# Layer 0 of a two-layer transformer kernel rebuilt: tokens tiled by head group, operands split into 12-bit halves, one ring of PSUM bank pairs

## The chip, the cores and the metric

The kernel runs on one core of one Trainium2 chip. The metric is the device time of one execution in microseconds (us); below full speed the profile gives the clock that was granted to TensorE as a share. The engines are called PE (TensorE; PEld are its weight loads), DVE (VectorE), ACT (ScalarE), POOL (GpSimd) and SP (SyncE, which only issues transfers).

## What is computed

Two layers over x of shape (2, 1024, 256), float32. Each layer normalizes x and adds an attention and a feed-forward network (FFN) of the same normalized input. The change touches layer 0 (layer 1 only in the order of its tokens):

```
def attn(x):                      # layer 0; b, t, e = 2, 1024, 256; h, d = 16, 16
    Q, K, V = ((x @ W.T).reshape(b, h, t, d) for W in (Wq, Wk, Wv))
    scores = causal(einsum('bhqd,bhkd->bhqk', Q, K))
    weights = softmax(scores / sqrt(d), axis=-1)
    ctx = einsum('bhqk,bhkd->bhqd', weights, V)
    return ctx.transpose(0, 2, 1, 3).reshape(b, t, e) @ Wp.T + bp
def ffn(x):
    w1, w2 = ternary(W_fc), ternary(W_proj)     # -s, 0 or s in groups of 64
    h = square(relu(x @ w1.T))                  # hidden width 1024
    return (h * rsqrt(mean(h * h) + eps)) @ w2.T
xn = layernorm(x)
x = x + attn(xn) + ffn(xn)
```

The reshape takes no transpose before it, so head h of a batch is made of the 64 tokens 64h to 64h+63, each cut into 16 pieces of 16 channels: 1024 positions of 16 numbers. Layer 1 is an attention with compressed keys and values and a second FFN.

## The kernel before

**Layout.** `x_sb` holds the 2048 tokens as 16 tiles of 128 consecutive ones. Layer 0 normalizes them, transposes them to channels by tokens (`xnT`, float32) and projects Q, K and V for a whole batch and 128 channels at a time (`project`, L252; float32, which PE runs as two records per matmul). A projection goes to DRAM ("rows") and comes back by `gather` (L279) in another order: for one *group* g of four heads (h4, h4 + 4, h4 + 8, h4 + 12 of a batch; eight groups in all) the heads lie at partitions 0, 32, 64 and 96, 16 rows each. This *quad* arrangement lets four matmuls with a contraction of 16 rows run side by side in PE's array (`tile_position`). A copy, mostly on POOL (L292), puts the positions of the gathered tile in order.

**The loop.** Everything in layer 0 runs under `tc.manual_schedule()`, so each engine executes its instructions in the order in which the loop writes them. The loop runs over groups g = -1 to 8 and over twelve *rounds* n. Round n takes a block of queries or keys of a width from `WIDTH` (512, 384, 256, 128, four times 512, and again 512, 384, 256, 128), in two *half-rounds* of two quads each. A half-round does two things at once, each with two of the four quads: `maxima` (L320) of group g + 1, that is, scores by query row, of which DVE takes the row maximum (L343 where no mask is needed, L338 with one); and `scores` (L358) of group g, that is, scores by key row, of which ACT takes exp (L375) and POOL clears the masked triangle (L378). `finish` (L347) transposes the negated maxima on PE (L352) and adds them to a 17th row of the queries, so that the scores come out with the maximum already subtracted. `product` (L386) multiplies weights and values two rounds later, in two parts where it is wide; `close` (L408) divides by the sum, and `project_out` (L423) applies Wp.

**PSUM.** Of eight banks, scores have two pairs (tag "s"), the product one bank ("o"), and three single banks ("m") serve maxima, transposes, FFN and output projection in turn.

**FFN.** `ffn` (L446) works on 512 tokens: eight `up` steps (L456; ReLU on ACT L462, square on DVE L463, sum of squares on POOL L468 and L469) and four `down` steps (L485; added to x at L492), the root of the mean square once per 512 tokens (L479). A list `fill` holds all of them with a cost, and a credit that the rounds earn decides when the next one is put in. The ternary weights are made in steps during g = -1 and 0 (`ternary`, L216).

**Order at the start.** All Q and K projections of batch 0 come first, then the gather of group 0, V, the gather of group 1, and batch 1's projections during g = -1.

Of the kernel before, what the change touches and what calls it, by code (L numbers as in the profile page):

```python
# [27 lines left out]
P = 128  # L28
# [22 lines left out]
def two_layers(ctx: ExitStack, tc: tile.TileContext, a: dict, out: bass.AP):  # L51
    nc = tc.nc
    x_d = a["x"].rearrange("(n p) e -> p n e", p=P)
# [8 lines left out]
    for g in range(4):  # L62
        nc.sync.dma_start(x_sb[:, 4 * g : 4 * g + 4, :], x_d[:, 4 * g : 4 * g + 4, :])
# [32 lines left out]
    def layernorm_T(scratch, xh, xl, ps_bank):  # L96
# [3 lines left out]
        for g in range(4):  # L100
# [7 lines left out]
            for n in range(4 * g, 4 * g + 4, 2):  # L108
# [12 lines left out]
                at = slice(n * P, (n + 2) * P)  # L121
                turned = pt.rearrange("p (c t) -> p c t", c=KC)
                nc.scalar.copy(xh[:, :, at], turned)
                nc.vector.tensor_tensor(xl[:, :, at], turned, xh[:, :, at], ALU.subtract)
# [12 lines left out]
    with ExitStack() as scope:  # L137
# [5 lines left out]
        GC = 4 * D0  # L143

        def ps_pair():
            return ps0.tile([P, 2, SC], F32, tag="s", name="ps_s", bufs=2)

        def ps_bank():
            return ps0.tile([P, SC], F32, tag="m", name="ps_m", bufs=3)

        def temp(name):
            return l0t.tile([P, SC], F32, tag="temp", name=name, bufs=6)

        wqkv = l0.tile([P, 3, KC, E], F32, tag="wqkv", name="wqkv")
        for i, key in ((1, "wk"), (0, "wq"), (2, "wv")):
            nc.scalar.dma_start(wqkv[:, i], a[key])
        wfc = l0.tile([P, KC, HID0], F32, tag="wfc", name="wfc")
        nc.gpsimd.dma_start(wfc, a["wfc"])
        wpr = l0.tile([P, HID0 // P, E], F32, tag="wpr", name="wpr")
        nc.gpsimd.dma_start(wpr, a["wpr"])  # L160
# [8 lines left out]
        nc.gpsimd.memset(half1[64:128, 64:128], 1.0)  # L169

        stage = []
        for i in range(3):
            t = l0.tile([P, H0, GC], F32, tag=f"stage{i}", name=f"stage{i}")
            nc.gpsimd.memset(t, 0.0 if i == 0 else 1.0)
            stage.append(t)

        nmx = []
        for k in range(2):
            t = l0.tile([P, TB, P], F32, tag=f"nmx{k}", name=f"nmx{k}")
            nc.gpsimd.memset(t, 0.0)  # L180
            nmx.append(t)

        xnT = main.tile([P, KC, B * S], F32, tag="xnT", name="xnT0")
        mv = l0.tile([P, NT, 2], F32, tag="ln_mv", name="ln_mv")
        rstd = l0.tile([P, NT], F32, tag="ln_rstd", name="ln_rstd")

        def ln_stats(g):
            for n in range(4 * g, 4 * g + 4):
                st = small.tile([P, 6], F32, tag="ln_st", name="ln_st")
                nc.vector.bn_stats(st, x_sb[:, n, :])  # L190
                nc.vector.bn_aggr(mv[:, n, :], st)
            r = rstd[:, 4 * g : 4 * g + 4]
            nc.scalar.activation(r, mv[:, 4 * g : 4 * g + 4, 1], AF.Sqrt, bias=eps["ln"])

        def ln_rstd(g):
            r = rstd[:, 4 * g : 4 * g + 4]
            nc.vector.reciprocal(r, r)

        def ln_turn(n):

            pt = ps_bank()
            for k in range(2):
                xn = l0t.tile([P, E], F32, tag="xn", name="xn", bufs=3)
                nc.vector.tensor_scalar(
                    xn, x_sb[:, n + k, :], mv[:, n + k, 0:1], rstd[:, n + k : n + k + 1],
                    ALU.subtract, ALU.mult,
                )
                for kc in range(KC):
                    nc.tensor.transpose(
                        pt[:, (2 * kc + k) * P : (2 * kc + k + 1) * P],  # L210
                        xn[:, kc * P : (kc + 1) * P], ident,
                    )
            nc.scalar.copy(xnT[:, :, n * P : (n + 2) * P], pt.rearrange("p (c t) -> p c t", c=KC))


        def ternary(w):  # L216
# [3 lines left out]
            def begin():  # L220
                t["wb"] = l0t.tile([P, SC], BF16, tag="q_wb", name="q_wb", bufs=1)
# [30 lines left out]
        def project(b, i, m, n=None):  # L252
            if (b, i, m) not in pend:
                pend[b, i, m] = ps_pair()
# [370 lines left out]

# [486 lines left out]
```

## Time and profile before

| what | value |
|---|---|
| median of 3 runs (lowest, highest) | 1468.72 us (1468.25, 1474.49) |
| the profiled execution | 1462.64 us |
| its span, first to last instruction | 1460.9 us |
| layer 0: start to the first maxima (L327) | 0 to 64.7 us |
| maxima of group 0 alone (g = -1) | 64.7 to 124.2 us |
| groups 0 to 6: scores of g, maxima of g + 1 | 124.2 to 564.6 us |
| group 7: scores alone | 564.6 to 605.6 us |
| last output projection ends | 615.4 us |
| layer 1 | 615.4 to 1460.9 us |
| mean granted clock of PE | 0.925 |

A line of the profile names the line of the kernel, the engine, the operation, what it writes and reads (`out<-in`) with shapes, how often it ran, its busy time, the mean duration of one in ns, and after the second bar the idle time of its engine just before it and what ended that. A timeline line has start, duration, engine, line, operation and tiles. In a table of stretches each engine's busy time is followed by its number of instructions. Matmuls overlap, and one that waits for a free bank can look busy.

### The profile page before, as it was taken

How to read it: one execution, taken by the hardware profiler on the slowest of the kernel's cores; microseconds unless marked ns; L12 is line 12 of the kernel's file. 1: busy time of each engine (PE TensorE's matmuls, PEld its weight loads, DVE VectorE, ACT ScalarE, POOL GpSimd, SP SyncE). 2: the span in 40 equal slices, each digit the busy share in tenths (PEclk: the TensorE clock that was granted, in tenths of full speed). 3: DMA queues.
4: the chain of work that ended last, by engine and by line, in shares of the span. 5: the costliest groups of instructions: out<-in, count | busy, mean ns of one | idle time of the engine just before them, and what ended most of it. 6: DMA issues, size and time to landing. Idle time of an engine off the chain costs nothing.

```text
span 1460.9 us, 36203 instructions
## 1 busy us (share of the span) xinstructions
PE 1355.2 (93%) x15382; PEld 818.7 (56%) x15382; DVE 828.3 (57%) x2161; ACT 591.5 (40%) x1131; POOL 530.3 (36%) x557
## 2 busy tenths in 40 slices
PE   5799999999999999865996899999999999999998
PEld 2334354354455344354874566767668566766676
DVE  2366555554554653273241577777665877776654
ACT  1113444443443544322330544444455544444453
POOL 2258671540612331127430532232345321323342
PEclk9786899998999999677996999999999999999999
DMA  5311000100100000130006000000000000000000
GB/s 193 105 57 45 1 22 1 23 21 2 23 1 9 1 1 1 42 95 0 30 29 162 8 3 14 3 14 13 13 14 24 4 11 13 11 6 13 13 13 20
DMA packets 56578, 39.26 MB, mean 27 GB/s; under 512 B 36896, under 2 KB 52512, under 8 KB 56064
## 3 DMA queue, kind: packets, MB, share of 16 engines
q1 hardware_dynamic: 50800, 29.47, 6.9%
q10 hardware_dynamic: 4944, 3.41, 0.8%
q0 software_dynamic: 672, 4.06, 0.7%
q8 instruction: 121, 1.98, 0.6%
q14 instruction: 41, 0.34, 0.1%
HBM read 24.35 MB, written 10.49 MB: 24 GB/s over the span
## 4 chain that ended last, share of the span: by engine, by line
PE 80%; DVE 6%; POOL 4%; issue 4%; ACT 3%; DMA 2%; ACTq 0%; SPq 0%; DVEq 0%; POOLq 0%
PE ps_s L921 17%; PE ps_m L327 13%; PE ps_o L965 11%; PE ps_t L870 7%; PE ps_o L398 5%; PE ps_m L485 5%; PE ps_m L456 4%; PE ps_t L989 4%; PE ps_s L259 4%; PE ps_s L368 2%; DVE p L927 2%; PE ps_o L755 1%; PE ps_m L435 1%; PE ps_t L954 1%; POOL qa L766 1%
## 5 line engine op out<-in xcount | busy, mean ns | idle before, releaser
L934 ACT ACTIVATE p<-p,nmax 128x1024 f32<-128x1024 f32 (+7 forms) x256 | 198.4, 775 | 326.3 <-DVE nmax L927 324.0
L921 PE MATMUL ps_s<-kT,qc 128*128 128x512 f32 (+3 forms) x768 | 307.1, 511 | 7.4 <-DVE nmax L927 7.0
L327 PE MATMUL ps_m<-head,head 16*128 16x512 f32 (+3 forms) x768 | 231.5, 571 | 6.9 <-DVE nmx L338 4.7
L375 ACT ACTIVATE p<-ps_s 128x1024 f32<-128x1024 f32 (+1 forms) x192 | 154.2, 810 | 199.0 <-PE ps_s L368 194.7
L939 DVE STREAM_TRANSPOSE pT<-p 128x1024 f32<-128x1024 f32 (+7 forms) x256 | 197.8, 772 | 0.2 <-ACT p L934 0.2
L921 PEld LDWEIGHTS ps_s<-kT,qc 128*128 128x128 f32 x768 | 125.6, 189 | 110.1 <-issue 64.7
L368 PE MATMUL ps_s<-head,head 17*128 17x512 f32 (+3 forms) x768 | 182.8, 587 | 1.0 <-ACT p L375 1.0
L965 PE MATMUL ps_o<-pT,vrep 32*64 32x128 f32 x9216 | 181.8, 279 | 1.9 <-DVE xT L974 1.8
L965 PEld LDWEIGHTS ps_o<-pT,vrep 32*64 32x64 f32 x9216 | 137.7, 130 | 70.8 <-issue 62.2
L888 POOL TENSOR_TENSOR qc<-t,t 32x512 f32<-32x512 f32 x128 | 161.8, 1264 | 8.2
L327 PEld LDWEIGHTS ps_m<-head,head 16*128 16x128 f32 x768 | 88.7, 193 | 119.8 <-issue 44.3
L946 POOL COPY rb<-rinv 128x512 f32<-128x512 f32 x32 | 19.6, 611 | 372.8 <-DVE rinv L944 338.2
L927 DVE CUSTOM_DVE_ANT_0 p<-ps_s,zeros 128x512 f32<-128x512 f32 x128 | 87.6, 684 | 70.5 <-PE ps_s L921 70.0
L378 POOL TENSOR_SCALAR_AFFINE_SELECT p<-p 128x256 f32<-128x256 f32 x128 | 55.0, 441 | 170.6 <-ACT p L375 170.2
L927 DVE CUSTOM_DVE_ANT_0 p<-ps_s,maskz 128x512 f32<-128x512 f32 (+3 forms) x128 | 62.3, 486 | 77.7 <-PE ps_s L921 77.5
L343 DVE TENSOR_REDUCE nmx<-ps_m 128x1 f32<-128x512 f32 x128 | 82.6, 686 | 34.8 <-PE ps_s L368 30.1
L398 PE MATMUL ps_o<-p,v 128*32 128x512 f32 (+4 forms) x920 | 93.8, 483 | 0.6 <-POOL p L378 0.5
L927 DVE CUSTOM_DVE_ANT_0 p<-ps_s,maskz,nmax 128x512 f32<-128x512 f32 (+3 forms) x128 | 70.5, 551 | 19.5 <-PE ps_s L921 2.6
L338 DVE CUSTOM_DVE_ANT_0 junk<-ps_m,maskz,nmx 128x512 f32<-128x512 f32 (+3 forms) x128 | 65.5, 548 | 28.2 <-PE ps_s L368 19.8
L456 PE MATMUL ps_m<-xnT,wfc 128*128 128x512 f32 x128 | 74.2, 709 | 1.3 <-DVE nmx L338 1.3
L884 POOL TENSOR_TENSOR t<-t,sinq 128x512 f32<-128x512 f32 x32 | 40.7, 1270 | 91.1 <-ACT t L883 87.4
L338 DVE CUSTOM_DVE_ANT_0 junk<-ps_m,maskz 128x512 f32<-128x512 f32 (+3 forms) x128 | 57.5, 486 | 24.7 <-PE ps_s L368 13.6
(185 smaller groups left out, 1944.1 us busy)
## 6 DMA issues: line engine op xcount, KB each, us to landing
rows<-proj SPq DMA_DIRECT2D x12, 512.0 KB, 2.6
stage<-rows SPq DMA_DIRECT2D x96, 64.0 KB, 2.4
x_sb<-in_x SPq DMA_DIRECT2D x4, 512.0 KB, 11.4
wo<-in_wo SPq DMA_DIRECT2D x8, 256.0 KB, 3.1
x<-x_sb SPq DMA_DIRECT2D x4, 512.0 KB, 2.8
xin<-x SPq DMA_DIRECT2D x16, 128.0 KB, 3.1
out<-xin SPq DMA_DIRECT2D x16, 128.0 KB, 1.7
w<-in_w ACTq DMA_DIRECT2D x2, 768.0 KB, 5.0
```

Of the source, the lines that this page charges most:

```text
L327: nc.tensor.matmul(t[:, :w], quad(q, c, D0)[:, i * P : (i + 1) * P], quad(k, c, D0)[:, k0 : k0 + w], start=True, stop=True, tile_position= ...
L338: nc.vector.tensor_tensor_reduce(junk[:, :w], t[:, :w], maskz[:, SC - w :], -1.0, dst if k0 else 3.0e38, ALU.add, ALU.min, dst,)
L368: nc.tensor.matmul(t[:, c % 2, :w], quad(k, c, D0 + 1)[:, j * P : (j + 1) * P], quad(q, c, D0 + 1)[:, at : at + w], start=True, stop=True, ...
L375: nc.scalar.activation(p[:, pair[0] : pair[0] + 2, :w], t[:, :, :w], AF.Exp)
L398: nc.tensor.matmul(quad(box["o"], c)[:, SC - w + lo : SC - w + hi], values[g][:, j, 32 * c : 32 * c + 32], p[:, c, lo:hi], start=(j == 0), ...
L456: nc.tensor.matmul(ph, wfc[:, kc, hc * P : (hc + 1) * P], xnT[:, kc, n * SC : (n + 1) * SC], start=(kc == 0), stop=(kc == KC - 1),)
L888: nc.gpsimd.tensor_tensor(qc[b, i][64 + 32 * x : 96 + 32 * x, g, hh], t1[at : at + 32], t2[at : at + 32], ALU.add,)
L921: nc.tensor.matmul(sc[:, : n1 - n0], qc[s.b, s.i][:, s.g, h // QP, h % QP, :], kT[:, s.b * S + n0 : s.b * S + n1], start=True, stop=True,)
L927: nc.vector.tensor_tensor_reduce(s.p[:, n0:n1], sc[:, : n1 - n0], mask, -1.0, 3.0e38 if n0 == 0 else s.nmax, ALU.add, ALU.min, nmax,)
L934: nc.scalar.activation(p[:, :w], p[:, :w], AF.Exp, bias=nmax, scale=-1.0, accum_out=rsum)
L939: nc.vector.transpose(s.pT[:, : s.nsb, h, :], p[:, : 32 * s.nsb])
L965: nc.tensor.matmul(s.o[64 * hh : 64 * hh + 64, c, : QP * 32], vrep[32 * c : 32 * c + 32, s.b * 32 + sb, :], s.pT[32 * c : 32 * c + 32, sb, ...
```

## The change

**Token order.** A tile pair of `x_sb` now holds the 256 tokens of one group of heads. x is loaded by 32 DMAs of 64 tokens from SP's and ACT's queues. Projection, attention and FFN of layer 0 all work per group of 256 tokens. Layer 1 gets its usual order back when it transposes, and reads and writes by strided access.

**Halves.** The normalized input and the Q, K and V weights are split into two float32r parts, a 12-bit upper half and the rest (`xh`, `xl`, `halves`). A projection is four products of halves, one record each. For Q and K both halves go through DRAM and come back stacked: 16 rows of upper and 16 of lower halves per quad, 32 in all. Head times head gives upper x upper plus lower x lower; a second matmul against a copy with the halves exchanged (`swap`, eight DMAs from SBUF to SBUF, or for group 0 a second gather) gives the mixed terms. Scores have a third matmul, a row of ones against the split maxima (`top`). V is projected with tokens as rows, and its heads are gathered by four DMAs straight into `values`.

**PSUM.** Maxima and scores take bank pairs from one ring of three ("ms"). One bank ("m") serves all else, one ("o") the products, which are no longer split.

**FFN.** Weights are float32r (a ternary value fits into one half), inputs and hidden values are halves. Each group has four `up` and four half `down` steps. Square and sums move to POOL and ACT, and the reciprocal root is made from ScalarE's Ln and Exp with one correction step on DVE, once per group.

**Order.** A dictionary `plan` puts each step at a fixed place: group, round, after the first ("x1") or second ("x2") half-round; what such a step still has to do on DVE or ACT is done by `settle` after the next half-round's reductions and exps. Projections of groups 0 and 1 come before the loop, of 2 to 4 in g = -1, of 5 to 7 in groups 0 to 2.

```diff
         def ps_pair():
-            return ps0.tile([P, 2, SC], F32, tag="s", name="ps_s", bufs=2)
+            return ps0.tile([P, 2, SC], F32, tag="ms", name="ps_ms", bufs=3)
...
-            return ps0.tile([P, SC], F32, tag="m", name="ps_m", bufs=3)
+            return ps0.tile([P, SC], F32, tag="m", name="ps_m")
...
+        def project(g, i, bank=ps_bank, lower=nc.gpsimd):
+
+            pw = bank()
+            for m in range(2):
+                four_ = [(kc, x, s) for kc in range(KC) for x in (xl, xh) for s in (1, 0)]
+                for n, (kc, x, s) in enumerate(four_):
                     nc.tensor.matmul(
...
+            nc.scalar.activation(t[:, 0, :].bitcast(F32R), pw, AF.Copy, scale=scale)
+            if lower is nc.vector:
...
+                nc.scalar.activation(t[:, 1, :], pw, AF.Copy, scale=scale)
+                nc.gpsimd.tensor_tensor(t[:, 1, :], t[:, 1, :], t[:, 0, :], ALU.subtract)
...
+                st = l0t.tile([P, H0, GC], F32, tag="stage", name="stage", bufs=1)
+            src = rows[g, i].rearrange("s m (j d) t -> s d (m j) t", d=D0)
             for c in range(4):
...
+                for s in range(2):
+                    lo = 32 * c + D0 * s
+                    q.dma_start(st[lo : lo + D0], src[1 - s if swapped else s, :, :, at])
...
+            for c in range(4):
+                for s in range(2):
+                    lo, of = 32 * c + D0 * s, 32 * c + D0 * (1 - s)
+                    nc.sync.dma_start(swapped[lo : lo + D0].bitcast(F32), t[of : of + D0])
...
+            for c in range(4):
+                src = rows[g, 2][c // 2, GC * (c % 2) : GC * (c % 2) + GC, :]
+                src = src.rearrange("t (j d) -> (t j) d", d=D0).rearrange("(k p) d -> p k d", p=P)
+                nc.sync.dma_start(values[g % 2][:, :, c, 0:D0], src)
...
+            k, q = heads[g, 1], (heads[g, 0], heads[g, 0, "swapped"])
+            t = ps_pair()
+
+            def run(part):
+                for c in pair:
+                    nc.tensor.matmul(
+                        t[:, c % 2, :w], quad(q[part], c)[:, i * P : (i + 1) * P],
+                        quad(k, c)[:, k0 : k0 + w],
+                        start=(part == 0), stop=(part == 1), tile_position=(32 * c, 0),
+                    )
...
+                if k0 + w < (i + 1) * P:
+                    nc.vector.tensor_reduce(
+                        peak(g)[:, i, pair[0] : pair[0] + 2], t[:, :, :w], AX.X, ALU.max, negate=True
+                    )
+                    return
...
+                    if part < 2:
+                        of, by = quad(k[part], c)[:, j * P : (j + 1) * P], quad(q, c)[:, at : at + w]
+                    else:
+                        of, by = quad(onesr, c, 2), quad(tops[g, iq], c, 2)[:, SC - w :]
...
+            whole = l0t.tile([P, SC], F32, tag="whole", name="whole", bufs=1)
+            nc.scalar.activation(whole, ph, AF.Relu)
+            nc.gpsimd.tensor_tensor(whole, whole, whole, ALU.mult)
...
+                nc.scalar.copy(t[:, 0, :], whole)
+                nc.scalar.activation(sq, whole, AF.Square)
+                nc.gpsimd.tensor_tensor(t[:, 1, :], whole, t[:, 0, :], ALU.subtract)
+                if j:
+                    nc.gpsimd.tensor_tensor(acc, acc, sq, ALU.add)
...
+            def add():
+                if k == 0:
...
+                    nc.scalar.activation(r, v, AF.Ln)
+                    nc.scalar.activation(r, r, AF.Exp, scale=-0.5)
...
+        for g in range(NG):
+            at(g, 0, "x1", lambda u=g: down(u, 0, 0))
+            at(g, 0, "x2", lambda u=g: down(u, 0, 1))
+            at(g, 1, "x1", lambda g=g: box["turn", g, 1]())
+            at(g, 2, "x1", lambda u=g: down(u, 1, 0))
+            at(g, 2, "x2", lambda u=g: down(u, 1, 1))
...
+            at(g, 7, "x1", lambda g=g: close(g, 0))
+        for g in range(-1, NG - 1):
+            at(g, 5, "x1", lambda g=g: box["turn", g + 1, 0]())
+            for j in range(4):
+                at(g, 8 + j, "x2", lambda u=g + 1, j=j: up(u, j))
+        for g in range(3):
+            at(g, 4, "x2", lambda g=g: project(g + 5, 1))
+            at(g, 5, "x2", lambda g=g: project(g + 5, 0))
+            at(g, 6, "x2", lambda g=g: project_v(g + 5))
...
+                        for r in range(3):
+                            for runs, _ in both:
+                                if r < len(runs):
+                                    runs[r]()
+                        for _, f in both:
+                            f()
+                        settle()
+                        if part == 0 and k >= 0:
+                            product(k // 12, k % 12)
+                        place(g, n, "x2" if part else "x1")
...
                             nc.tensor.matmul(
                                 pw[:, i * SC : (i + 1) * SC], w[:, kc, hc * P : (hc + 1) * P],
-                                x[:, kc, n * SC : (n + 1) * SC],
+                                x[:, kc, n * SC : (n + 1) * SC].rearrange(
+                                    "p (c h t) -> p h c t", c=2, h=4
+                                ),
```

As built, the instruction stream of the changed kernel has a table load before each of the eight Ln and each of the eight Exp of the FFN.

## The prediction

> **What bounds the kernel now.** I read the busy shares first, then a table of stretches cut where layer 0 changes its work (first maxima at 64.7 us, first scores at 124.2, last maxima at 564.6, last product at 605.6), then the timeline of one round, then the groups of instructions.
>
> ```profile
> PE 1355.2 (93%) x15382; PEld 818.7 (56%) x15382; DVE 828.3 (57%) x2161; ACT 591.5 (40%) x1131; POOL 530.3 (36%) x557
> ```
> ```profile
> core 0: us, PE busy (x) PEld busy (x) DVE busy (x) ACT busy (x) POOL busy (x), PEclk, DMA share, GB/s
> 0.00:64.70 64.70, 37.34 (x96) 18.04 (x96) 20.30 (x57) 10.03 (x16) 10.97 (x27) 0.89 0.41 146
> 64.70:124.20 59.50, 56.45 (x149) 24.15 (x149) 35.88 (x91) 10.18 (x14) 36.89 (x34) 0.76 0.23 74
> 124.20:564.60 440.40, 433.65 (x2770) 201.04 (x2768) 243.06 (x682) 186.96 (x255) 184.20 (x216) 0.92 0.05 11
> 564.60:605.60 41.00, 39.34 (x240) 13.88 (x236) 2.74 (x8) 20.01 (x28) 6.83 (x17) 0.71 0.00 1
> ```
> TensorE is busy throughout the loop, and nobody else is above 55% of it. Seven groups take 440.4 us, 62.9 each; the last, with scores alone, takes 41.0.
>
> ```profile
> 300.73 0.70 PE L327 MATMUL ps_m<-head,head 16*128 16x512 f32 x2
> 300.74 0.70 PE L368 MATMUL ps_s<-head,head 17*128 17x512 f32 x2
> 301.26 0.59 PE L327 MATMUL ps_m<-head,head 16*128 16x512 f32 x2
> 301.27 0.59 PE L368 MATMUL ps_s<-head,head 17*128 17x512 f32 x2
> 301.80 0.64 PE L398 MATMUL ps_o<-p,v 128*32 128x256 f32 x8
> 302.37 1.26 PE L327 MATMUL ps_m<-head,head 16*128 16x512 f32 x3
> 302.94 0.70 PE L368 MATMUL ps_s<-head,head 17*128 17x512 f32 x2
> ```
> One float32 matmul is two records, and four quads run side by side: a half-round of 512 columns takes 301.80 - 300.73 = 1.07 us. The third maxima record then stands from 302.37 to 302.94 for a bank that VectorE frees: a "busy" PE can be a waiting one. The same timeline gives 0.85, 0.62 and 0.41 us for 384, 256 and 128 columns: 0.054 us per pass and 128 columns, plus 0.1 per set of records. A group's 24 half-rounds make 12 x 1.06 + 4 x (0.85 + 0.62 + 0.41) = 20.2 us. Products (0.99, 0.78, 0.57, 0.36 by width) make 9.4 and their splits 1.1, FFN up 16 x 0.48 = 7.7, down 32 x 0.228 = 7.3, six blocks of four transposes 3.6, the sums of squares 0.5: 49.8 us. Of the 13 left to 62.9, five are the granted clock (0.92), some two the output projection; the rest, six, is waits for banks.
>
> Float32r, as the change uses it, is in layer 1's FFN:
>
> ```profile
> 705.05 3.12 PE L755 MATMUL ps_o<-w3t,hid 128*128 128x256 f32 x24
> 708.01 0.40 PE L740 MATMUL ps_wide<-xl,w2t 128*128 128x512 f32 x1
> 708.24 0.39 PE L740 MATMUL ps_wide<-xh,w2t 128*128 128x512 f32 x1
> ```
> One record per matmul, every 0.23 us for 512 columns and 2.96/24 = 0.123 for 256. The drains of a round:
>
> ```profile
> L343 DVE TENSOR_REDUCE nmx<-ps_m 128x1 f32<-128x512 f32 x112 | 72.3, 686 | 32.9 <-PE ps_s L368 30.1 <-PE ps_m L327 2.1
> L338 DVE CUSTOM_DVE_ANT_0 junk<-ps_m,maskz,nmx 128x512 f32<-128x512 f32 x28 | 19.9, 748 | 5.7 <-PE ps_s L368 4.0 <-PE ps_m L327 1.6
> L375 ACT ACTIVATE p<-ps_s 128x1024 f32<-128x1024 f32 x84 | 85.9, 1024 | 109.1 <-PE ps_s L368 106.3 <-POOL p L378 1.5 <-POOL acc L469 1.2
> L469 POOL TENSOR_TENSOR acc<-acc,sq 128x512 f32<-128x512 f32 x28 | 35.9, 1281 | 2.2
> L479 ACT ACT_TABLE_LOAD x4 | 5.1, 1283 | 0.1
> ```
>
> **The change, part by part, for a group at full clock.** Maxima and scores: three sets of one pass instead of two sets of two. Per half-round 3 x 0.054 per 128 columns plus 0.2 (today's) to 0.3 (0.1 per set); the middle gives 0.90, 0.74, 0.58, 0.41, so 17.7 us (16.5 to 18.9): only 2.5 saved, since the third set, which brings the maximum in, eats most of it. Products 9.4 (no splits). Up and down: 32 records each of 0.123, 3.9 and 3.9, and 0.95 for the sums of squares now made in every group: 6.7 saved. Four blocks of transposes 2.4 (values come through a DMA). Sum 38.3. In groups 0 to 2 three projections of 16 records add 5.9; today all projections lie before group 0.
>
> The waits: the ring of three pairs is handed out as maxima, scores, maxima, and so on; the scores of a half-round take the pair of the maxima one half-round before, so their first set waits for that reduction. Without a mask it is one instruction of 128x1024, not in this trace: at least one L343 (0.69), at most two (1.37); VectorE's copy of that size out of PSUM (L272) took 1.22, which I take as the nearest. Masked ones follow each other every 0.67, 0.54, 0.40, 0.27 us, two per half-round. Matmul end to VectorE's start and back adds 0.27 (0.17 of it the fill within a record). Against this stand the last score set (0.15 to 0.3), the product (first half) and whatever the plan puts there. Half-rounds with too little: rounds 4 to 7 without projections (0.6 + 1.2, 0.2 + 1.2, 0.2 + 1.2, 1.2), rounds 1 and 3 (1.1, 0.7), rounds 8 and 9 (0.8): about 8 us per group, 5 where projections fill in.
>
> A second wait is new: the transposes of the maxima in round 1 need the one bank "m", which holds the first FFN output until it is added. That add waits behind two reductions, exp (0.81), a table load (L479's 1.28), Ln (0.26), a second load (1.28), Exp (0.26), four small VectorE operations (0.6) and the add (0.48): some 5.6 us after the maxima, covered by 0.6 of PE work. Queued behind the transposes stands the whole of TensorE; behind Ln every exp. I take 5 us in each of 8 groups (bounds 0, were the loads hidden, and 7). Smaller waits for "m" behind ScalarE's copies: 1.5.
>
> Other engines per group: ScalarE 24 exps 19, FFN 12 x 0.6, copies 2.4, tables 3, projections 3: 35. POOL 16 selects 6.8, 11 FFN operations (1.05 to 1.28) 13.4, two permutes of 1.98, bias 1.5, lower halves 2.5: 28. VectorE 28. SP issues 39 DMAs of 0.45: 17. All lie beside PE's 44, if their order holds. The copies of the lower halves and the 64-byte value gathers have some 30 us of cover; uncovered, a gather of 8 issues plus 2.4 to land would cost 6 us.
>
> The clock: low in stretches of quads and products with few full-array matmuls; in layer 1's float32r stretch 708 to 736 us it is 1.00. Between 0.92 and 1.00 I take 0.95: 2 us per group. Groups 0 to 2: 38.3 + 5.9 + 5 + 5 + 1.5 + 2 = 57.7; 3 to 6: 38.3 + 8 + 5 + 1.5 + 2 = 54.8; output projection, mostly inside ring waits, 2 in all. Sum 394, against 440.4 (bounds: 7 x 38.3 + 17.7 = 286 without any wait; 448 with today's 62.9 and 1 more).
>
> Before the loop: SP and ScalarE now issue 35 loads; ScalarE's 18 (0.45 to 0.5) end near 10 us and hold its first square root until 11.5, so the first transposes stay near 13. Two projections, rows out, then 16 gathers of 0.5 on ScalarE's queue, behind a wait for the rows at 26: until 35 the next group's root and copy stand behind them, and VectorE and PE behind those. Then a chain of transposes, copies, four projections, ternary steps: first maxima near 58 (48 to 66) against 64.7. Next stretch: maxima in two sets 12.6, nine projections 17.7, up 3.9, transposes and scales 4.6: 38.8, at a clock of 0.9 and with POOL at 40 us taken as 45 (39 to 56) against 59.5. Last group: scores 17.7, products 9.4, down 4.9, transposes and output 6.6, the chain 5, and 3.5 for the clock (0.71 today): 47 (38 to 56) against 41.0. Tail: 8 against 9.8. Layer 1, 845.5 us from 615.4, has only its addresses and eight stores changed: nothing, hidden behind matmuls (0 to 3).
>
> Sum: 58 + 45 + 394 + 47 + 8 + 845.5 = 1397.5 of span against 1460.9. 1.7 us lie around the span, and the median of the runs is 6.1 above the profiled 1462.6: 1405 us.
>
> **The skill against the trace.** The trace has VectorE's reductions at 0.69 us per 512 columns whatever TensorE does. The Trainium skill (TensorEngine Tiling, PSUM Bottleneck) says that tiling speeds TensorE up but not the emptying of PSUM; that speaks against this change, and taken strictly (every half-round at reduction plus hand-over, some 43 us per group before all else) it gives about what I have for the ring. In the last group PE is busy 39.34 of 41.00 us at a granted 0.71. The skill (TensorE: Matmul & The Clock Gate, What's actually happening) says that a busy array is released to the full clock; the trace differs, and by the page the last group would be some 3 us shorter than I say.
>
> **Rivals.** (1) The waits are covered: half the ring's and the chain's cost gone, groups of 46 to 48, loop 330, first maxima at 50: near 1325. For it: table loads run ahead of their wait (L479's did). Against: nothing but 0.6 us lies in front of round 1's transposes. (2) POOL leads in rounds 8 to 11: two selects and three FFN operations, 4.4 us, against PE's 3.3, and "whole" has one buffer, so the next ReLU waits for POOL and the exps behind it: 4 x 1.1 x 8 groups = 35: 1440. Against: rounds 4 to 7 leave POOL nearly idle. (3) Slower: the ring. If the hand-over costs 0.9 us a half-round more, because ScalarE or the settling adds stand in front of the reductions, 24 x 0.9 x 7 = 150: 1555; it decides from 65 us per group on, where the loop's growth eats the 17 us won around it. For it: ScalarE at 35 of 55 us. Against: today VectorE starts within 0.1 us of the records' end. (4) The single passes bring nothing in quads: half-rounds stay 1.06, 3 more per group, 1430; layer 1's rows speak against it.
>
> **How the numbers follow.** Forecast (1360 to 1425) 0.45; rival 1 0.20; rivals 2 and 4 0.20; rival 3 0.12 slower, and 0.03 within half a per cent (7 us, about what a measurement here can tell from no change). Faster 0.83 to 0.85, rounded down for what I overlooked: 0.82, same 0.03, slower 0.15. Range 1320 to 1470, from rival 1's lower part to where rival 2's cost is met by a late first maximum.
>
> **What would show it.** Groups 55 to 58 us apart (by the transposes of the maxima); one PE stall near 5 us per group there; a half-round of 512 columns in 0.85 to 0.95 us; first maxima at 48 to 66 us; clock above 0.92. A group over 65 us, with PE waiting for the reductions, makes the forecast wrong; so does one under 48.

## The result, and the profile after

The changed kernel took 1556.74 us (median of 4 runs, 1548.56 to 1562.0) beside 1470.83 for the kernel before on the same chip: 1.058 of it, 95% interval 1.052 to 1.064. It is slower; the forecast was 1405. The profiled execution has a span of 1560.3 us. (The 1468.72 given ahead is the median of three runs of the kernel before, 1470.83 that of four.)

The first line is the busy shares on the page, the others the table of stretches, cut at the same events as before (first maxima, first scores, last group's first scores, last output projection); after each stretch stand its length, the busy time of each engine, the granted clock and the DMA share.

```profile
PE 1312.1 (84%) x15998; PEld 890.1 (57%) x15998; DVE 818.2 (52%) x2113; ACT 654.7 (42%) x1247; POOL 538.5 (35%) x575
```
```profile
core 0: us, PE busy (x) PEld busy (x) DVE busy (x) ACT busy (x) POOL busy (x), PEclk, DMA share, GB/s
0.00:82.00 82.00, 21.60 (x116) 18.21 (x116) 27.30 (x53) 16.62 (x28) 19.76 (x35) 0.79 0.41 112
82.00:170.60 88.60, 54.49 (x297) 40.21 (x296) 41.93 (x111) 22.00 (x41) 39.15 (x32) 0.68 0.34 82
170.60:641.90 471.30, 398.82 (x3141) 242.31 (x3140) 219.04 (x618) 225.43 (x326) 173.65 (x220) 0.78 0.21 40
641.90:703.00 61.10, 49.25 (x358) 29.21 (x358) 6.28 (x18) 28.86 (x42) 14.55 (x26) 0.81 0.00 1
703.00:1560.30 857.30, 787.96 (x12091) 560.12 (x12089) 523.66 (x1315) 361.81 (x811) 291.38 (x265) 0.94 0.08 24
```

PE went from 93% to 84% busy, and what is left runs at a lower clock: 0.78 in the loop, against 0.92. Every stretch is longer than before:

| us | before | forecast | after | after less forecast |
|---|---|---|---|---|
| to the first maxima | 64.7 | 58 | 82.0 | 24.0 |
| g = -1 | 59.5 | 45 | 88.6 | 43.6 |
| groups 0 to 6 | 440.4 | 394 | 471.3 | 77.3 |
| group 7 and tail | 50.8 | 55 | 61.1 | 6.1 |
| layer 1 | 845.5 | 845.5 | 857.3 | 11.8 |
| span | 1460.9 | 1397.5 | 1560.3 | 162.8 |

**Before the loop.** ACT's timeline (start, duration, engine, line; "ACTq" is the issuing of transfers):

```profile
4.12 18.70 ACTq L67 DMA_DIRECT2D x_sb<-in_x  x13
24.21 0.29 ACT L240 ACTIVATE ln_rstd<-ln_mv,eps_ln 128x2 f32<-128x2 f32 x1
38.98 9.26 ACTq L349 DMA_DIRECT2D ctx_n<-rows  x16
48.29 0.29 ACT L240 ACTIVATE ln_rstd<-ln_mv,eps_ln 128x2 f32<-128x2 f32 x1 [13.43 <-DMA ctx_n<-rows]
```

Thirteen loads of x hold the queue for 18.7 us, 1.4 each: the chain of waits shows the issue itself standing for earlier loads (12.3 us at one of them). The first square root comes at 24.2; the next group's stands behind rows and gathers until 48.3.

**In g = -1** the waits of PE name one source first, POOL's normalized input (two operations of 1.22 us on a queue that also does ternary steps):

```profile
PE ps_e L256 <- POOL xn L249: 13.2, 4, 6.3
PE ps_m L256 <- POOL xn L249: 11.8, 4, 8.0
```

**In the loop** the list of PE's waits (total us, times, longest) is led by the transposes of the maxima:

```profile
PE ps_m L438 <- DVE x_sb L607: 33.8, 7, 5.3
PE ps_ms L459 <- DVE peak L413: 9.7, 14, 1.0
PE ps_ms L459 <- DVE peak L420: 7.4, 14, 0.7
PE ps_m L577 <- POOL h L563: 7.1, 6, 1.2
PE ps_m L577 <- ACT whole L552: 6.6, 7, 1.2
```

The timelines of PE, POOL and ACT in group 5, which starts at 509.4, show the sequence:

```profile
513.11 0.74 PE L577 MATMUL ps_m<-wpr,h 128*128 128x256 f32 x4
515.05 0.74 PE L577 MATMUL ps_m<-wpr,h 128*128 128x256 f32 x4 [1.19 <-POOL h L563]
516.28 1.76 PE L587 MATMUL ps_m<-ones,acc 128*128 128x1 f32 x8 [0.49 <-POOL acc L565]
519.23 0.66 PE L483 MATMUL ps_o<-p,v 128*32 128x128 f32 x8
524.64 1.09 PE L438 MATMUL ps_m<-ident,nmx 128*128 128x128 f32 x4 [4.75 <-DVE x_sb L607]
```
```profile
511.94 1.05 POOL L553 TENSOR_TENSOR whole<-whole 128x512 f32<-128x512 f32 x1
513.73 1.27 POOL L563 TENSOR_TENSOR h<-whole,h 128x512 fp32r<-128x512 f32 x1 [0.38 <-ACT h L561]
514.95 1.27 POOL L565 TENSOR_TENSOR acc<-acc,sq 128x512 f32<-128x512 f32 x1
```
```profile
520.17 1.28 ACT L599 ACT_TABLE_LOAD   x1
521.46 0.20 ACT L599 ACTIVATE rn<-rn 128x2 f32<-128x2 f32 x1
521.68 1.28 ACT L600 ACT_TABLE_LOAD   x1
522.98 0.20 ACT L600 ACTIVATE rn<-rn 128x2 f32<-128x2 f32 x1
```

Down waits for POOL, the sums take 1.76 us for eight records of one column, and the transposes wait 4.75 us for the add behind Ln and Exp. From 516 to 533 the granted clock is 0.5. Rounds 0, 1 and 2 take 9.1, 8.7 and 8.2 us (means over the seven groups) at clocks of 0.89, 0.53 and 0.56; the other nine rounds take 2.5 to 6.1 us.

### The profile page after: what moved, and what is told of

Read it like the earlier page. It is cut to its first block, busy times and chain, and to the rows that moved or that the text cites. A ratio compares the mean times of both kernels' runs of the same rounds, so it can differ in the third digit from the quotient of the medians.

```text
span 1560.3 us, 37942 instructions
## 1 busy us (share of the span) xinstructions
PE 1312.1 (84%) x15998; PEld 890.1 (57%) x15998; DVE 818.2 (52%) x2113; ACT 654.7 (42%) x1247; POOL 538.5 (35%) x575
## 3 DMA queue, kind: packets, MB, share of 16 engines
q1 hardware_dynamic: 102192, 43.90, 12.3%
## 4 chain that ended last, share of the span: by engine, by line
PE 66%; DVE 10%; POOL 9%; ACT 7%; issue 3%; DMA 3%; SPq 1%; ACTq 0%; DVEq 0%; POOLq 0%
PE ps_s L1062 16%; PE ps_o L1106 11%; PE ps_t L1011 7%; PE ps_ms L405 4%; PE ps_ms L459 4%; PE ps_o L483 4%; PE ps_t L1130 4%; PE ps_m L302 2%; PE ps_m L577 2%; POOL h L563 2%; DVE peak L413 2%; POOL acc L565 2%; POOL whole L553 2%; PE ps_m L528 1%; DVE p L1068 1%
## 5 line engine op out<-in xcount | busy, mean ns | idle before, releaser
L465 ACT ACTIVATE p<-ps_ms 128x1024 f32<-128x1024 f32 (+1 forms) x192 | 154.7, 809 | 198.7 <-PE ps_ms L459 197.5
L420 DVE CUSTOM_DVE_ANT_0 junk<-ps_ms,maskz 128x512 f32<-128x512 f32 (+3 forms) x128 | 62.8, 491 | 121.1 <-PE ps_ms L405 118.9
L413 DVE TENSOR_REDUCE peak<-ps_ms 128x2 f32<-128x1024 f32 x64 | 78.3, 1223 | 68.5 <-PE ps_ms L405 68.5
L459 PE MATMUL ps_ms<-head,head 32*128 32x512 f32 (+3 forms) x384 | 96.4, 511 | 17.9 <-DVE peak L413 9.7
L1068 DVE CUSTOM_DVE_ANT_0 p<-ps_s,maskz 128x512 f32<-128x512 f32 (+3 forms) x128 | 62.3, 486 | 81.2 <-PE ps_s L1062 81.0
L483 PE MATMUL ps_o<-p,v 128*32 128x512 f32 (+3 forms) x768 | 97.9, 589 | 0.4 <-ACT oT L489 0.4
L405 PE MATMUL ps_ms<-head,head 32*128 32x512 f32 (+3 forms) x384 | 94.4, 504 | 0.0
L420 DVE CUSTOM_DVE_ANT_0 junk<-ps_ms,maskz,peak 128x512 f32<-128x512 f32 (+3 forms) x128 | 70.5, 550 | 43.2 <-PE ps_ms L405 40.3
L405 PE MATMUL ps_ms<-head,swap 32*128 32x512 f32 (+3 forms) x384 | 81.9, 435 | 0.0
L405 PEld LDWEIGHTS ps_ms<-head,head 32*128 32x128 f32 x384 | 41.3, 218 | 64.8 <-issue 30.5
L459 PE MATMUL ps_ms<-top,onesr 2*128 2x512 f32 (+3 forms) x384 | 75.9, 397 | 0.0
```

The lines of the kernel that those rows point to most:

```text
L405: nc.tensor.matmul(t[:, c % 2, :w], quad(q[part], c)[:, i * P : (i + 1) * P], quad(k, c)[:, k0 : k0 + w], start=(part == 0), stop=(part == ...
L413: nc.vector.tensor_reduce(peak(g)[:, i, pair[0] : pair[0] + 2], t[:, :, :w], AX.X, ALU.max, negate=True)
L420: nc.vector.tensor_tensor_reduce(junk[:, :w], t[:, c % 2, :w], maskz[:, SC - w :], -1.0, dst if k0 else 3.0e38, ALU.add, ALU.min, dst,)
L459: nc.tensor.matmul(t[:, c % 2, :w], of, by, start=(part == 0), stop=(part == 2), tile_position=(32 * c, 0),)
L465: nc.scalar.activation(p[:, :, :w], t[:, :, :w], AF.Exp)
L483: nc.tensor.matmul(quad(box["o"], c)[:, SC - w :], values[g % 2][:, j, c, :], p[c // 2][:, c % 2, :w], start=(j == 0), stop=(j == 4 * iq + ...
```

## The experiments

All are edits of the changed kernel. Totals are medians, ratios are to the kernel before on the same chip. That kernel was itself at 1470.8 in the first session and near 1458 in the others, and the changed kernel was not timed again there, so a single step is read from the stretches of the profiled executions (us; "clock" is that of groups 0 to 6). A profile is of one execution. The loop has the same instructions in after, e4 and e7 and took 471.3, 461.2 and 468.6 us; so has group 7, with 46.3, 54.1 and 46.6. In these two columns a difference of less than some 10 us therefore shows nothing. The two columns ahead of them repeat within 3 us. e9's profile is of the slowest of its ten executions (1466.9). Where no edit is printed, the expectation names it.

| run | total | ratio (95%) | to maxima | g = -1 | groups 0-6 | group 7's scores | clock |
|---|---|---|---|---|---|---|---|
| after | 1556.7 | 1.058 (1.052 to 1.064) | 82.0 | 88.6 | 471.3 | 46.3 | 0.78 |
| e1_no_root | 1519.7 | 1.041 (1.034 to 1.048) | 82.9 | 90.1 | 444.2 | 40.9 | 0.79 |
| e2_fill | 1607.4 | 1.101 (1.089 to 1.114) | 82.4 | 90.2 | 520.5 | 56.4 | 0.77 |
| e3_replan | 1548.6 | 1.061 (1.054 to 1.068) | 81.7 | 88.6 | 453.3 | 50.6 | 0.84 |
| e4_xn_dve | 1548.5 | 1.061 (1.057 to 1.065) | 82.4 | 82.3 | 461.2 | 54.1 | 0.80 |
| e5_dense_fill | 1561.5 | 1.072 (1.056 to 1.087) | 81.4 | 88.6 | 464.9 | 48.4 | 0.87 |
| e6_down32 | 1538.5 | 1.056 (1.045 to 1.067) | 83.0 | 88.5 | 459.8 | 46.9 | 0.83 |
| e7_queues | 1537.6 | 1.056 (1.043 to 1.068) | 64.4 | 91.3 | 468.6 | 46.6 | 0.79 |
| e8_replan2 | 1525.5 | 1.047 (1.034 to 1.061) | 81.2 | 88.5 | 420.6 | 56.4 | 0.86 |
| e9_all2 | 1457.3 | 1.000 (0.998 to 1.003) | 64.1 | 60.2 | 411.8 | 63.1 | 0.85 |
| e10_all3 | 1438.7 | 0.988 (0.981 to 0.995) | 62.8 | 62.0 | 406.7 | 42.4 | 0.92 |
| e11_nudge | 1438.3 | 0.987 (0.982 to 0.992) | 62.9 | 62.6 | 402.2 | 47.2 | 0.89 |
| e12_all4 | 1437.2 | 0.987 (0.982 to 0.991) | 62.7 | 60.6 | 405.3 | 44.7 | 0.92 |

**Is the clock low because PE stands still?** Two runs: the chain left out, and the stall filled.

```diff
-                    v, r, t = (small.tile([P, 2], F32, tag="rn", name="rn") for _ in range(3))
...
-                    fs["rn"] = r
+                    fs["rn"] = ones[:, 0:2]
```

> Leaves out the reciprocal root of the FFN: Ln, Exp and the four small VectorE steps; the factor is taken as one, the sums of squares are still made. Theory A (the chain from the sums to the add holds the one bank, and TensorE's stand in front of the transposes of the maxima also costs it the granted clock afterwards): the stall of 4.8 us per group falls below 1.5, the clock in rounds 1 and 2 rises from 0.5 to above 0.8, a group takes 57 to 62 us instead of 67.3, total 1475 to 1515 against 1557. Theory B (the clock is low because of what TensorE executes there, not because of the stall): only the stall goes, 8 x 4 = 32 us, total 1520 to 1530, clock still near 0.5.

```profile
PE ps_m L438 <- DVE x_sb L597: 6.8, 7, 1.4
```

The stall fell from 33.8 to 6.8 us in the loop and a group to 63.5, 3.9 less; but rounds 1 and 2 still ran at 0.53 and 0.57. The chain costs about what was forecast, and the clock is another matter: this is theory B by its clock, and the total (1519.7) meets the lower end of B's range.

```diff
...
+                nc.tensor.matmul(
+                    po[:, 3 * P : 4 * P], wpr[:, 0, 0:P], onesr, start=fresh, stop=fresh
+                )
...
```

> Adds work and takes nothing away: 12 full-array float32r matmuls of 128 columns ahead of the second half of down, and 48 behind the sums of squares, into unused columns of the bank that down holds, so that TensorE is busy while it waits. Theory A (the clock follows TensorE's idle time): the clock of the loop rises from 0.78 to above 0.88, rounds 1 and 2 run near full speed, a group falls from 67.3 to 59 to 64 us although it executes some 5 us more; total 1500 to 1535. Theory B: the clock stays at 0.78, total 1555 to 1580.

Theory A falls. The matmuls took longer than the stall (75.2 us in the loop, against 33.8 of stall), so the total is above theory B's range too; and with PE busy from 554.7 to 561.5 without a gap the clock stayed at 0.5. The twenty us that begin there, in the view of stretches of e2 (PE busy 16.96 of 20.50, clock 0.50):

```profile
554.70:575.20 20.50, 16.96 (x97) 13.57 (x98) 3.31 (x16) 5.31 (x8) 1.14 (x3) 0.50 0.00 1
```

**What the clock follows.** I then counted, for windows of 3.41 us (the step in which the trace changes the granted clock), what the array did: columns streamed times rows/128 times columns in use/128, a float32 record twice (it takes 0.2325 us for 256 columns, a float32r one 0.123), over 8192, a scale on which the densest rows, 512 columns in 0.23 us, come to 0.92. 1.0 on it is called the array's capacity. Over all fourteen kernels, layer 0 from 60 to 600 us:

| work in a window | windows | next window at 1.0 |
|---|---|---|
| below 0.34 | 673 | 0 |
| 0.34 to 0.36 | 90 | 4 |
| 0.36 to 0.38 | 113 | 59 |
| 0.38 to 0.40 | 104 | 99 |
| 0.40 and more | 1235 | 1226 |

PE's busy share does not separate the two: of 827 windows followed by 0.5, 264 were over 95% busy; of 1388 followed by 1.0, 270 were under 90%. e2's fill came to about 0.25: its 48 matmuls of 128 columns follow each other every 0.2 us, and the weight loads beside them are busy all that time (9.38 us).

```diff
...
-                    po[:, 3 * P : 4 * P], wpr[:, 0, 0:P], onesr, start=fresh, stop=fresh
+                    po[:, 260:SC], wpr[:, 0, 0:P], wfc[:, 0, 260:SC], start=fresh, stop=fresh
...
```

(The edit is shown against e2.)

> As e2_fill, with as many columns in fewer and wider matmuls: 6 and 24 of 252 columns instead of 12 and 48 of 128. In all kernels so far the granted clock of a window of 3.41 us is 1.0 after a window in which TensorE's array did more than 0.37 of what it can do at full speed (columns streamed, times the share of rows and columns in use; a float32 record counts twice), and 0.5 after one with less, however long PE was busy; e2's matmuls, held up by their weight loads, come to 0.25. Theory D (this work decides): the wide ones come to 0.4 even at half clock, so rounds 1 and 2 rise from a clock of 0.53 and 0.57 to above 0.8, round 2 falls from 8.2 to below 6 us, a group from 67.3 to 61 to 65, total 20 to 40 us below e2's successor without fill (1557). Rival (a fixed time of low clock after each stall): clock in rounds 1 and 2 stays below 0.65, total above 1555.

Nearly as many columns, half as many matmuls (32.0 us of PE in the loop instead of 75.2): the clock of round 1 went from 0.53 to 0.83 and the loop's from 0.78 to 0.87. Round 2 stayed at 0.55, which is the rival's clock, and the total did not fall, which is the rival's total: the added work costs 32.0 us, and the loop is only 6.4 shorter. The count by windows holds in this run as in the others (3 of 159 windows on the wrong side of 0.37), but the fill covers only part of the stall: the transposes still wait 21.7 us in the loop, and behind that wait the windows are thin again (from 317.9 us on 0.24, 0.31 and 0.36, followed by 0.5 each time). The mechanism holds, the size I expected does not.

```diff
...
-                for s in (1, 0):
...
-                        po[:, :E], fs[u, hc // 2][:, s, lo : lo + P], wpr[:, hc, :],
...
+                    po[:, :E], fs[u, hc // 2][:, 0, lo : lo + P], wpr[:, hc, :].bitcast(F32),
...
```

> The second FFN matmul in float32 again: the hidden values stay whole (no copy on ACT, no subtraction on POOL), 16 float32 matmuls instead of 32 float32r ones of halves, twice the passes: 7.4 us of PE per group at full clock instead of 3.9. Theory D: the longer work lifts the array's share in rounds 0 to 2, the clock there rises from 0.5 to 0.6 to above 0.8, POOL's sums come 5 us earlier, a group takes 58 to 63 us, total 1480 to 1520. Rival (passes cost what they cost): groups 67 to 71, total 1555 to 1585.

Twice the passes in down and no loss: the clock of rounds 0 to 2 is at 0.98, 0.75 and 0.66 instead of 0.89, 0.53 and 0.56. The loop is 11.5 us shorter than in after but only 1.4 shorter than in e4, so a gain is not shown. A group takes 65.7 us, between the two ranges. The total moved less than I expected; the stall at the transposes (35.2 us in the loop) stayed.

**Where the steps stand.**

```diff
-            at(g, 0, "x1", lambda u=g: down(u, 0, 0))
...
-            at(g, 1, "x1", lambda g=g: box["turn", g, 1]())
...
+            at(g, 0, "x1", lambda g=g: box["turn", g, 1]())
...
+            at(g, 2, "x2", lambda u=g: root(u))
+            at(g, 4, "x1", lambda u=g: down(u, 0, 0))
...
```

> Same work, other places: transposes of the maxima in round 0, sums of squares and the root by themselves in round 2 (the bank is free at once), down in rounds 4 to 6, up half a round earlier, projections in rounds 1, 3 and 7. Theory A: TensorE no longer waits for POOL's sums nor for the root, a group takes 54 to 60 us, loop clock above 0.88, total 1460 to 1510. Rival C (POOL, which works on the hidden values through rounds 8 to 11, and ScalarE behind it set the pace wherever TensorE's steps are put): groups stay above 64 us, total above 1530, with the waits moved to the exps or to up's bank.

```profile
PE ps_ms L459 <- DVE peak L420: 33.1, 36, 3.5
```

Half of it: the loop fell by 18 us. The waits for POOL's sums are gone, the longest for the add is 1.5 us, but waits for the masked reductions rose to 33.1 us (7.4 in after). The group (64.8 us) and the total are what rival C named, but not by its cause: the waits are neither at the exps nor at up's bank. Up and down now followed a first half-round, as the product does, and nothing stood after the second. This is the ring's wait, which the forecast put at 5 to 8 us a group; in after it is 17.1 us in seven groups.

> e3_replan with one job after every second half-round, where no product stands: there e3 had put down and up after the first half-round, beside the product, and TensorE then waited 1.1 to 1.2 us for VectorE's reductions between second and first half-rounds (33 us in the loop). Maxima turned in round 0, close in 1, root in 2, down in 3 to 6, the other turn in 7, up in 8 to 11, all after the second half-round. Theory: those waits fall below 15 us, a group takes 54 to 59 us at a clock above 0.88, loop 380 to 415 us instead of 453 (e3), total 1490 to 1515. Rival: POOL's hidden-value steps in rounds 8 to 11 return as the wait, groups above 61.

```profile
PE ps_ms L459 <- DVE peak L420: 3.9, 8, 1.0
```

With one job after each second half-round these waits fell to 3.9 us and the loop to 420.6, 20 below the kernel before. The loop and the total are still 6 and 10 us above the ranges of the theory. The largest wait left was 12.6 us, a transposition behind close.

**The two stretches ahead of the loop.**

```diff
-            load_x(g, nc.sync, nc.scalar)
+            load_x(g, nc.gpsimd)
...
-            gather(0, 0, more[:, 0], nc.scalar)
-            gather(0, 0, more[:, 1], nc.scalar, True)
+            gather(0, 0, more[:, 0])
+            gather(0, 0, more[:, 1], swapped=True)
```

> Before the loop: the loads of x for groups 4 to 7 go to POOL's queue instead of SP's and ACT's, and the 16 gathers of group 0 on ACT's queue go to SP's. Theory: ACT's first square root moves from 24.2 to 10 to 14 us, its 13 us of standing behind rows and gathers go, first maxima at 58 to 66 instead of 82, total 1533 to 1542. Rival: the gathers in a row on SP (24 of 0.6) or POOL's queue hold the first maxima above 74.

```profile
4.12 9.57 ACTq L67 DMA_DIRECT2D x_sb<-in_x  x5
15.08 0.29 ACT L240 ACTIVATE ln_rstd<-ln_mv,eps_ln 128x2 f32<-128x2 f32 x1
```

First maxima at 64.4; the first root comes at 15.1. The 17.6 us lost there were the transfers in front of ACT's work. The run moves loads and gathers together, and takes loads off SP's queue as well, so it does not divide the 17.6 among them.

```diff
-            at(-1, 5 + k if k else 0, "x1", lambda k=k: ln_turn(4 + k, nc.gpsimd))
+            at(-1, 5 + k if k else 0, "x1", lambda k=k: ln_turn(4 + k, nc.vector))
```

> In the stretch of the first maxima (g = -1) the normalized input of groups 4 to 7 is made on VectorE (0.42 us each) instead of POOL (1.22 each). Theory: TensorE's 25 us of waits for it in that stretch fall below 8, the stretch from 88.6 to 68 to 75 us, total 1537 to 1545. Rival: the stretch is held by the drains and the projections' copies, it shrinks by less than 5 us.

Only 6.3 us: PE's wait of 25.0 us fell to 18.6, since on VectorE the same step stood behind reductions and ternary steps. Both ranges are missed. e4 alone does not show what was late; e9, which makes the same input on the same engine but issues it ahead of its transposes, waits 3.4 us for it in that stretch. So the place counts for more than the engine.

**Together.** e9 takes e7's queues and e8's places (corrected), and issues the normalized input and the first ternary step ahead of their use; e10 adds e6's float32 down.

```diff
-            at(-1, 5 + k if k else 0, "x1", lambda k=k: ln_turn(4 + k, nc.gpsimd))
+            at(-1, 5 + k if k else 0, "x1", lambda k=k: ln_turn(4 + k))
+            if k < 3:
+                at(-1, 4 + k, "x2", lambda k=k: normed.update({5 + k: ln_scale(5 + k, nc.vector)}))
```

> All remedies together: the queues of e7; in g = -1 the normalized input on VectorE one half-round ahead of its transposes and the ternary steps' first part one round ahead; and e8's places once more, with the other turn of the maxima moved to round 9, root to 1, close to 2 (e8's wait of 12.6 us behind close goes) and the output projection's transposes set so that no group's context is overwritten before it is read (in e8 two of its tiles were). If the losses of the change are the four places found (queues, POOL's chain in g = -1, the two waits in rounds 0 and 1, the clock that follows them), they add up: first maxima 62 to 66, g = -1 at 72 to 80, loop 400 to 420, last group 50 to 56; total 1450 to 1480, so 0.99 to 1.015 of before. Rival: they hide one another (what one stretch wins, the next waits for): above 1500.

> e9 with e6's float32 down besides (hidden values whole, POOL and ACT two steps less per up, PE 3.5 us more per group at full clock). Theory D (work in the array pays for its clock): the clock of the loop rises by 0.05 or more over e9 and the loop is not longer, g = -1 is 4 to 8 us shorter because up no longer waits for the split; total 5 to 20 us under e9. Rival: in rounds 3 to 6, where TensorE now has enough to do, the passes cost 3 us a group: 15 to 25 us over e9.

The remedies add up: e9 is level with the kernel before, and e10, with more passes, is 18.6 us under e9 and 1.2% under the kernel before (0.988, interval 0.981 to 0.995). Not all of it came as expected: g = -1 in e9 is 12 us better than its range and the last group 7 us worse, and in e10 g = -1 is no shorter. Between e9 and e10 the loop differs by 5 us, which shows nothing. Group 7, which has the same scores and products in both, differs by 20.7 and shows how. The stretch of its scores in e9, e10 and e11:

```profile
536.10:599.20 63.10, 60.10 (x310) 32.98 (x309) 4.30 (x14) 27.12 (x38) 14.18 (x25) 0.59 0.00 1
```
```profile
531.50:573.90 42.40, 40.87 (x310) 23.21 (x310) 4.97 (x13) 24.80 (x34) 11.01 (x21) 1.00 0.00 1
```
```profile
527.70:574.90 47.20, 44.20 (x324) 25.87 (x323) 4.21 (x14) 26.97 (x38) 14.14 (x25) 0.93 0.00 1
```

PE is busy in all of them; the clock (the column ahead of the last two) is 0.59, 1.00 and 0.93. One half of a down, eight records each, in the timelines of e9 and of e10:

```profile
559.83 2.08 PE L584 MATMUL ps_m<-wpr,h 128*128 128x256 f32 x8
```
```profile
556.29 1.99 PE L581 MATMUL ps_m<-wpr,h 128*128 128x256 f32 x8
```

Here float32r at half clock takes as long as float32 at full clock.

```diff
+            pt = ps_bank()
+            for _ in range(14):
+                nc.tensor.matmul(pt, wpr[:, 0, 0:P], wfc[:, 0, 0:SC], start=True, stop=True)
...
+        at(NG - 1, 2, "x1", extra)
```

> e9 with 14 full-array float32r matmuls of 512 columns more, once, in round 2 of the last group; their result goes into a free bank and is not read. In e9's last group PE is busy throughout at a clock of 0.5 (63.1 us), its array doing 0.24 to 0.35 of its full-speed capacity in each window, because half the clock can hardly do more with this work; in e10 the same scores and products run at 1.0 and do 0.50 to 0.76. Theory D: one window of dense work tips the clock, and the rest of the group then keeps it up by itself: last group 44 to 52 us at a clock above 0.75 although 3.3 to 6.5 us of work is added, total 10 to 18 us under e9. Rival (e10's last group is faster because ACT and POOL have less to do, or by chance): 66 to 70 us at 0.5 to 0.6, total 3 to 6 us over e9.

With fourteen matmuls that nobody needs, e9's group 7 is 16 us shorter and the kernel, by the medians, 19 us. e9's windows from 546.8 to 591.2 hold 0.23 to 0.35 and stay at 0.5; e11 has 0.45 in the window of the added work, then 1.0, and 0.46 to 0.77 in the windows after it. The stretch at 0.5 in e9, and the added matmuls and the stretch behind them in e11:

```profile
546.80:591.20 44.40, 44.40 (x199) 22.93 (x199) 3.08 (x10) 16.89 (x21) 4.32 (x9) 0.50 0.00 1
```
```profile
540.20 4.34 PE L659 MATMUL ps_m<-wfc,wpr 128*128 128x512 f32 x14
```
```profile
546.00:574.90 28.90, 28.90 (x231) 16.09 (x229) 2.76 (x6) 15.43 (x20) 5.37 (x12) 1.00 0.00 1
```

The same stream holds itself at either clock. This is the plainest evidence that the clock follows the array's work: nothing was taken away. Not all of the difference between the two profiles is the added work's: ahead of it, where the instructions are the same, e11's loop is already 9.6 us shorter than in e9's slowest execution. The medians (1457.3 of ten runs, 1438.3 of four, each beside the kernel before at 1458.1) stand clear of that. And e11, with the cheap passes, is level with e10: the extra passes are not needed for that time.

> e10 with down moved forward to rounds 1 to 4, where the array has least to do (e10's clock there is 0.64 to 0.81), root to 0, both close to 5 and 6, and VectorE's four small steps after the root issued two half-rounds later, so that the reductions of the maxima don't stand behind ScalarE's two table loads (in e10 VectorE stands 3.5 us there). Theory D: clock in rounds 1 to 3 above 0.85, groups 53 to 57 instead of 54 to 62, total 10 to 25 us under e10. Rival: POOL's sums are not ready in round 0 and TensorE waits there for 2 to 3 us a group: total within 10 us of e10 or over it.

The rival came: the total is e10's. In round 0 PE waits up to 1.6 us for the bank (8.5 us in six groups), less than the rival named; in the chain of waits a square, the copy of the maxima and an exp on ScalarE stand in front of it, and POOL in front of the square. PE then runs the one-column sums; the clock falls to 0.57 in round 1, and the float32 down that was moved there takes 3.8 us for eight records instead of 2.0. Rounds 2 to 7 are at 0.9 to 1.0, and it evens out.

## Why the prediction was wrong

- **The clock, the step that failed most.** The forecast took 0.95, "2 us per group", between the loop's 0.92 and layer 1's float32r rows at 1.00, and 0.9 in g = -1. Measured: 0.78 and 0.68. In the loop this is the term that outweighs all others. The forecast's 394 us are some 302 of work, 14 of them for the clock, and 92 of waits (ring 47, chain 35, copies 10.5); measured are 399 us with PE busy and 72 without. By the windows, 165 of the busy us ran at 0.5. At full clock they would take about half, so up to 82 us are the clock's: an estimate, and an upper bound, since a matmul that waits for a bank looks busy. The working had the material: it saw that quads and products go with a low clock, before's own row for g = -1 has 0.76, and then it counted the halved passes only as time saved. They are also work taken out of the array: after's windows in the loop lie on both sides of the bound. e6 and e10 show it, where passes put back cost nothing or win, and e11, where added work alone wins. The count also fits the last group of the kernel before, busy at 0.71: from 580 to 604 us its windows hold 0.19 to 0.40 and run at 0.5. The Trainium skill (TensorE: Matmul & The Clock Gate, What's actually happening) lets the full clock follow one busy window of about 3.4 us and the low one an idle one. The window's length agrees with the 3.41 us here; "busy" does not, if it is read as PE's busy time: e2 and e9 were busy throughout at 0.5. It has to be read as work in the array.
- **The wait behind the root was right in place and price** (5 forecast, 4.8 measured; 3.9 per group in e1). The sentence "nothing but 0.6 us lies in front of round 1's transposes" held; what was left out is that the clock stays low in the work behind it.
- **Rival 2 was set against the wrong evidence.** POOL's chain is paid not in rounds 8 to 11 but in round 0, where down needs the last up's halves and sums, which POOL ends 6.8 and 8.0 us after that up began (508.2, 515.0, 516.2 in group 5); that rounds 4 to 7 leave POOL idle does not help. In after it is 16.6 us of waits (L577, L587): 10.0 for POOL's own results and 6.6 for the last ReLU, which in turn waits for POOL (6.7 us in the loop). The low clock begins there.
- **The ring was over-sized.** 2.4 us of waits per group instead of 5 to 8, and rival 3, whose time (1555) came nearest, did not happen: VectorE's reductions do not lead. e3 shows the wait that it would have been. So the group over 65 us that the forecast named as its sign came (67.3), without the wait named beside it. At full clock, half-rounds of 512 columns took 0.89 us, as forecast.
- **Before the loop** the issue of a load was priced at 0.45 to 0.5 us from before's queue, where three were issued; with eighteen on the queue the last thirteen take 1.4 each, and these 18.7 us stand ahead of the first root (24.0 us of error, 17.6 of them shown by e7).
- **g = -1** was summed from PE's work. Its 43.6 us of error are the clock and what PE waits for at POOL and ACT: PE is idle for 34.1 us there (25.0 for POOL, 9.0 for ACT), where the forecast left 2, and busy for 54.5 where it had 43. e9, with both steps issued ahead and the other places, has 60.2; what the other 15 us over the forecast are was not divided.
- **Layer 1** "nothing": 11.8 us. Set beside before's, its instructions lose 3.2 us at a transfer of weights and some 6 in the last 30 us, where the clock is low on the same instructions (below); the rest are small steps.

The single passes themselves did what the sum says; rival 4 is out.

## What to carry to other kernels

When a change makes TensorE's work cheaper, ask what it does to the work per 3.4 us, not only to the busy time: below about 0.37 of the array's capacity here, the clock halves, and at half the clock a thin stream can stay there (44 us in e9). So price a stall by what runs slowly after it, put dense matmuls where the stream is thin, and weigh the cheap pass against the clock where the array is not full. With one bank shared by many steps, place each step where its releaser is done, and put one job behind every half-round that has none.

## What the runs showed beyond this

The clock can differ where nothing else does. Near the end of layer 1, where the instructions are the same but for addresses, PE is as busy, 93 us apart; the stretches of after and of before:

```profile
1532.30:1536.30 4.00, 4.00 (x70) 2.54 (x69) 1.57 (x9) 1.26 (x5) 0.00 (x0) 0.50 0.02 4
```
```profile
1439.30:1443.30 4.00, 4.00 (x81) 3.16 (x81) 1.98 (x10) 2.25 (x9) 0.00 (x0) 1.00 0.00 0
```

Which windows a short wait falls into seems to decide it; that was not tried by itself. The 9 windows of 1235 over 0.40 that were followed by half the clock hang on how a matmul that crosses a window's edge is shared out: with its work spread evenly over its record, none of 1226 is, and 0.37 separates all but 32 of 2216 windows.
